# The tail of a four-layer network rearranged: another neighbour for the last convolution, a third of the depthwise chains on ScalarE and GpSimd, more PSUM banks

## The chip, the cores and the metric

The kernel runs on one core of one Trainium2 chip. The metric is the time of one execution on the device in microseconds (us), a median over several runs. Below, a number of a stage comes from the trace of one profiled execution, and a ratio is the mean time of one kernel's fast runs over the mean time of the other's fast runs of the same rounds, so it is not quite the quotient of the two medians quoted beside it. All runs told here were in the fast state, that is, none took over 1.5% longer than the fastest of its kernel on its chip. SBUF is the memory in which the kernel's tiles lie, PSUM the one into which its matmuls write, and a bank is here a PSUM buffer of 512 fp32 numbers for each partition; the granted clock is the share of full speed that the profile records for TensorE.

Three of the four calls for experiments went to chips on which every kernel takes some 1,000 us longer (the kernel before 9792 to 9833 us there, against 8717 to 8729 on the others). Where that time lies can be read in the traces: the part before the tail, with the gathers, ends at about 8100 us instead of 7050, and the last stage of the tail agrees to about 2 us between the chips (208.5 and 208.5 us in two kernels that share it). So every experiment is compared by the lengths of its tail stages, and by its ratio to the kernel before of its own rounds. The same saving in us gives a ratio about a tenth nearer to 1 on a slow chip, and the scatter of the part before the tail, which ended between 8101 and 8137 us in eight profiles on the slow chips, is in every ratio and in no tail.

## The reference, cut to what matters

Four images of 256 channels, 64 x 64 pixels, go through four layers in fp32:

```python
def reference(x, ...):                     # x: (4, 256, 64, 64)
    # layer 0: 1x1 convolution, deformable sampling (gathers), feed-forward
    # layer 1: linear attention over q, k, v and their aggregated copies
    qkv = relu(conv1x1(x) * scale + bias)                 # 768 channels
    agg = depthwise_5x5(qkv) + bias                       # the 25-tap chains
    agg = depthwise_1x1(agg) + bias
    ...                                                   # relu(q), relu(k), v k^T, projection, + x
    # layer 2: 3x3 convolution with binarised weights, + x
    # layer 3: attention over max-pooled keys: theta, phi (1024 keys), softmax, g, projection, + x
    return x
```

Group normalisations stand between the layers, folded into weights. One image depends on no other.

## The kernel before: the parts that matter

Images follow each other through a pipeline. While one image's points are gathered (GpSimd and DMA), another's layer 1 and a third's layers 2 and 3 run on the other engines. Generators yield costs, and `beside` advances several of them in proportion. After the gathers of the last image comes the tail: nothing is left to gather, and image 3 still has its feed-forward part, layer 1, layer 2 and layer 3 to do.

```python
def ps(self, name="ps"):                                   # every small product of TensorE
    return self.mm.tile([P, 512], F32, name=name, tag="mm")   # three PSUM banks rotate
...
def depthwise(self, acc, src, w, k, rows, cols, r0, bias=None, step=...):
    for t in range(k * k):                                 # a chain of 25 taps on VectorE
        s = src[:, r0 + t // k:r0 + t // k + rows, t % k:t % k + cols]
        wt = w[:, t:t + 1]
        if t:
            nc.vector.scalar_tensor_tensor(acc, s, wt, acc, ALU.mult, ALU.add)
        elif bias is not None:
            nc.vector.tensor_scalar(acc, s, wt, bias, ALU.mult, ALU.add)
        ...
        if t % 3 == 2 or t == k * k - 1:
            yield step(3.9)
...
def aggregate(pd, i, name, func, **more):                  # in layer 1, 24 times an image
    acc = self.ps1.tile([P, 16, W], F32, name="agg", tag="agg")     # the one PSUM buffer (two banks)
    yield from self.depthwise(acc, pd, self.w5[:, i], 5, 16, W, 0, bias=..., step=step)
    v = bp.tile([P, 16, W], F32, name=name, tag="ag", bufs=3)
    nc.scalar.activation(v, acc, func, **more)             # the copy that frees "agg"
    yield step(2)
    return v
...
# layer 3, one step of 128 tokens
s = [self.ps("s") for _ in range(2)]
for i in range(2):
    nc.tensor.matmul(s[i], tv[...], ph[...])               # score
    nc.vector.tensor_reduce(mx[:, i:i + 1], s[i], AX.X, ALU.max)
...
    nc.scalar.activation(pe[...], s[i], AF.Exp, bias=mx[:, 2:3], accum_out=...)
...
    nc.tensor.transpose(pt[:, m], pe[...], self.ident)     # then ScalarE copies pt to pT
...
    nc.tensor.matmul(ps[:, 0:P], pT[:, m], gt[:, m], ...)  # product
nc.vector.tensor_scalar(m2[...], ps[:, 0:P], den[:, 2:3], None, ALU.mult)
...
# the tail, in run()
def second(n):
    yield from self.layer2(n, ...)                         # 3x3 convolution
    yield from self.layer3(n, ...)                         # pooled attention
beside(range(64), 64, *behind(N - 1), (second(N - 2), SECOND, 0.2, 1))   # feed-forward and layer 1 of image 3
for _ in second(N - 1):                                                  # ... and then 3's layers 2, 3 alone
    pass
```

## Time and profile before

| kernel before | us |
|---|---|
| median of the runs (8709.94 to 8736.27) | 8729 |
| profiled execution | 8707 |
| of this, tail: end of image 3's feed-forward part to the end | 1669 |
| - layer 1 of image 3, beside layers 2 and 3 of image 2 | 1087 |
| - from there to the last matmul of image 3's convolution | 278 |
| - pooled attention of image 3, alone | 304 |

The borders are the starts of the last matmul of feed-forward's second layer, of layer 1's projection and of the convolution (each of these matmuls takes 0.6 us). Tails are given this way throughout. The prediction uses round borders a few us away (7044, 8150, 8404), so its stages differ by that.

This is the head of the page of the kernel before.

```profile
span 8706.8 us, 92673 instructions
PE 6339.9 (73%) x35276; PEld 3432.2 (39%) x35276; DVE 5243.8 (60%) x6279; ACT 2014.2 (23%) x4710; POOL 4578.5 (53%) x4694
```

No engine is above 73% over the whole, which says little: each stage has its own limit, and only the last fifth of the time is of concern. These groups are of the last stage of the kernel before (window 8404 to 8706). The columns: line, engine, operation, tiles, shapes, count; busy us and mean ns of one; idle time of the engine just before them, and what ended it.

```profile
L963 PE MATMUL ps<-gt,pT 128*128 128x128 f32 x512 | 76.0, 310 | 1.8
...
L958 PE MATMUL pt<-ident,pe 128*128 128x128 f32 x256 | 42.6, 291 | 63.4 <-ACT pe L950 63.0
```

TensorE idles 63 us in front of its transposes, as each waits for the exponentials. The matmuls themselves are recorded at 310 and 291 ns; the number matters later.

### The profile page before, as it was taken

The page shows a single profiled execution, that of the slowest core. Times are in us where ns is not written, and L with a number is a line of the kernel's source. Part 1 is how long each engine was busy: PE and PEld are TensorE (multiplying, and loading weights), DVE is VectorE, ACT ScalarE, POOL GpSimd, SP SyncE. Part 2 cuts the span into 40 slices and gives each one's busy share as a digit, 9 for nine tenths or more (in the row PEclk, how much of TensorE's full clock was granted, in tenths as well). Part 3 has the DMA queues.
Part 4 walks back from the last instruction along what each step waited for, and adds up shares of the span by engine and source line. Part 5 has one row for each costly group of instructions (what it writes and reads, how often), then busy time and mean ns, then how long its engine had stood idle before and what let it go on. Part 6 is the DMA issues. An engine that isn't in the chain of part 4 may idle for free. (4 is left out here: it accounts for less than half of the span.)

```text
span 8706.8 us, 92673 instructions
## 1 busy us (share of the span) xinstructions
PE 6339.9 (73%) x35276; PEld 3432.2 (39%) x35276; DVE 5243.8 (60%) x6279; ACT 2014.2 (23%) x4710; POOL 4578.5 (53%) x4694
## 2 busy tenths in 40 slices
PE   4645545569676677998767779897677898667887
PEld 2333322334333333444444434444444444334345
DVE  7445353342678775258777732778777268989213
ACT  1111111112222122222232322222322222222113
POOL 0667767677777776777776557777755000000000
PEclk7666766779767688999988989998888999889999
DMA  5556555554444454455544354555433211101210
GB/s 157 165 153 170 152 154 157 142 156 144 136 120 127 119 145 136 144 155 140 155 132 119 111 150 137 159 150 152 126 111 107 90 53 46 44 32 41 57 60 29
DMA packets 817660, 1052.57 MB, mean 121 GB/s; under 512 B 464064, under 2 KB 524608, under 8 KB 815424
## 3 DMA queue, kind: packets, MB, share of 16 engines
q0 software_dynamic: 225024, 614.77, 24.4%
q1 hardware_dynamic: 592192, 431.89, 17.3%
q8 instruction: 279, 4.57, 0.2%
q14 instruction: 165, 1.35, 0.0%
HBM read 878.36 MB, written 167.90 MB: 120 GB/s over the span
## 5 line engine op out<-in xcount | busy, mean ns | idle before, releaser
L520 POOL DMA_INDIRECT g<-tab,sl x4688 | 4577.8, 976 | 2169.9 <-issue 1295.2
L176 DVE SCALAR_TENSOR_TENSOR agg<-pad,vec,agg 128x1024 f32<-128x1024 f32 x2560 | 3295.3, 1287 | 69.1
L527 PE MATMUL acc<-g,wm 128*32 128x128 f32 x18752 | 1221.6, 319 | 1186.6 <-ACT at L532 762.0
L527 PEld LDWEIGHTS acc<-g,wm 128*32 128x32 f32 x18752 | 609.5, 121 | 1845.7 <-ACT at L532 984.7
L864 PE MATMUL ps<-xp,w 128*128 128x512 f32 x2304 | 1062.3, 608 | 80.7 <-DVE xp L848 52.8
L864 PEld LDWEIGHTS ps<-xp,w 128*128 128x128 f32 x2304 | 425.7, 192 | 565.5 <-issue 530.8
L552 ACT COPY dT<-dp 64x112 f32<-64x112 f32 x1176 | 287.1, 244 | 1328.9 <-PE dp L537 935.3
L511 DVE TENSOR_TENSOR wm<-con,sl 128x1024 f32<-128x1024 f32 (+1 forms) x296 | 357.5, 1208 | 223.5 <-PE acc L527 221.3
L645 PE MATMUL ps<-x2f,f 128*128 128x512 f32 x1024 | 477.3, 615 | 4.0 <-ACT f L636 4.0
L167 DVE SCALAR_TENSOR_TENSOR hm<-ps,vec,lk 128x512 f32<-128x512 f32 x256 | 192.2, 751 | 436.2 <-ACT lk L166 436.1
L652 PE MATMUL ps<-hm,f 128*128 128x512 f32 x1024 | 453.6, 597 | 0.0
L166 ACT ACTIVATE lk<-ps,low 128x512 f32<-128x512 f32 x320 | 219.8, 687 | 980.9 <-PE ps L645 558.2
L700 PE MATMUL ps<-xr,qw 128*128 128x512 f32 x768 | 418.1, 675 | 12.3 <-DMA xq<-x 3.2
L958 PE MATMUL pt<-ident,pe 128*128 128x128 f32 x1024 | 187.6, 330 | 228.2 <-ACT pe L950 226.1
L950 ACT ACTIVATE pe<-s,mx 128x512 f32<-128x512 f32 x256 | 173.8, 684 | 712.9 <-DVE mx L945 712.8
L414 PE MATMUL ps<-mw,t 128*128 128x108 f32 x512 | 96.5, 364 | 306.9 <-DVE t L404 306.9
L963 PE MATMUL ps<-gt,pT 128*128 128x128 f32 x2048 | 309.6, 314 | 5.6 <-ACT pT L959 3.1
L963 PEld LDWEIGHTS ps<-gt,pT 128*128 128x128 f32 x2048 | 287.9, 224 | 49.4 <-ACT pT L959 20.0
L653 DVE TENSOR_TENSOR xyf<-xyf,ps 128x512 f32<-128x512 f32 x64 | 44.0, 688 | 430.9 <-PE ps L652 430.9
L560 PE MATMUL po<-dT,ow 128*128 128x224 f32 (+1 forms) x1216 | 284.6, 383 | 24.6 <-DVE yb L564 13.2
L532 ACT COPY at<-acc 128x256 f32<-128x256 f32 (+1 forms) x588 | 218.5, 372 | 313.9 <-PE acc L527 304.8
L645 PEld LDWEIGHTS ps<-x2f,f 128*128 128x128 f32 x1024 | 192.1, 194 | 233.2 <-issue 224.5
(224 smaller groups left out, 7096.4 us busy)
## 6 DMA issues: line engine op xcount, KB each, us to landing
x<-x SPq DMA_DIRECT2D x160, 512.0 KB
g<-tab,sl POOLq DMA_INDIRECT x4688
xr<-x SPq DMA_DIRECT2D x96, 512.0 KB
x<-in_x SPq DMA_DIRECT2D x64, 512.0 KB
tab<-xo SPq DMA_DIRECT2D x512, 64.0 KB
y<-yc SPq DMA_DIRECT2D x32, 512.0 KB
x2f<-x SPq DMA_DIRECT2D x32, 512.0 KB
xyf<-x SPq DMA_DIRECT2D x32, 512.0 KB
```

The costliest lines, as they stand in the source:

```text
L166: nc.scalar.activation(t, ps, AF.Identity, bias=low, scale=SLOPE)
L176: nc.vector.scalar_tensor_tensor(acc, s, wt, acc, ALU.mult, ALU.add)
L511: nc.vector.tensor_tensor(wm[:, 0:nu], self.con("own").unsqueeze(1).unsqueeze(1).to_broadcast(sh), sl[:, r:r + nu, G:].unsqueeze(3).to_bro ...
L520: nc.gpsimd.indirect_dma_start(out=g[:, i, :], out_offset=None, in_=table, in_offset=bass.IndirectOffsetOnAxis(ap=sl.bitcast(I32)[:, r, i: ...
L527: nc.tensor.matmul(acc[32 * i:32 * i + 32, :], wm[:, r4, 4 * i + 2 * x:4 * i + 2 * x + 2, :], g[:, i, x * P:(x + 1) * P], start=x == 0, st ...
L552: nc.scalar.copy(dT[b][hs, :, q0:q0 + m * (v1 - v0)].rearrange("p g (v o) -> p g v o", o=m), dp[u][hs, v0:v1, :, s, 0:m].rearrange("p v g ...
L560: nc.tensor.matmul(po[m][:, 0:np_], self.ow[:, k, m * P:(m + 1) * P], dT[b][:, k, 0:np_], start=k == 0, stop=k == G - 1)
L645: nc.tensor.matmul(ps, f1[:, k, m * P:(m + 1) * P], x2[:, k], start=k == 0, stop=k == KT - 1)
L652: nc.tensor.matmul(ps, f2[:, k, m * P:(m + 1) * P], hm[:, k], start=k == 0, stop=k == 4 * KT - 1)
L700: nc.tensor.matmul(ps, qw[:, k, t * P:(t + 1) * P], x[:, k], start=k == 0, stop=k == KT - 1)
L864: nc.tensor.matmul(ps, w[:, k, t, m * P:(m + 1) * P], xp[:, k, t // 3:t // 3 + 8, t % 3:t % 3 + W], start=i == 0, stop=i == KT * 9 - 1)
L963: nc.tensor.matmul(ps[:, 0:P], pT[:, m], gt[:, m], start=m == 0, stop=m == 7)
```

## The change

The intent is to use the tail's idle engines. (1) Image 2's pooled attention no longer runs beside layer 1 but beside image 3's convolution, which had been alone. (2) The sampling's SBUF pools are closed before the tail, which makes room for more buffers. (3) In the tail every third aggregation chain is done by ScalarE (products) and GpSimd (sums). (4) More PSUM banks rotate, and pooled attention in the tail takes its scores in other banks ("wide"). The core of the diff:

```diff
-        return self.mm.tile([P, 512], F32, name=name, tag="mm")
+        tag = next(self.banks)
+        return (self.mm if tag == "mm" else self.ps1).tile([P, 512], F32, name=name, tag=tag)
...
+    def products(self, pool, acc, src, w, k, rows, cols, r0, bias, step):
+        for t in range(k * k):
+            s = src[:, r0 + t // k:r0 + t // k + rows, t % k:t % k + cols]
+            if t:
+                m = pool.tile([P, rows, cols], F32, name="m", tag="product", bufs=4)
+                nc.scalar.activation(m, s, AF.Copy, scale=w[:, t:t + 1])
+                nc.gpsimd.tensor_tensor(acc, acc, m, ALU.add)
+            else:
+                nc.scalar.activation(acc, s, AF.Identity, bias=bias, scale=w[:, t:t + 1])
+            if t % 3 == 2 or t == k * k - 1:
+                yield step(0.5)
...
+                turn += 1
+                if self.alone and turn % 3 == 2:
+                    acc = v = bp.tile([P, 16, W], F32, name=name, tag="av2")
+                    yield from self.products(bp, acc, pd, self.w5[:, i], 5, 16, W, 0, self.b5[:, i:i + 1], step)
+                else:
+                    acc = self.ps1.tile([P, 16, W], F32, name="agg", tag="agg")
...                                                        # pads and "ag": one buffer more when alone
-                    s = [self.ps("s") for _ in range(2)]
+                    if not wide:
+                        s = [self.ps("s") for _ in range(2)]
+                    elif j % 2:
+                        s = self.ps1.tile([P, 2, 512], F32, name="s", tag="agg")
+                        s = [s[:, i] for i in range(2)]
+                    else:
+                        s = [self.ps1.tile([P, 512], F32, name="s", tag=tag) for tag in ("acc", "dp")]
...
-        beside(range(64), 64, *behind(N - 1), (second(N - 2), SECOND, 0.2, 1))
-        for _ in second(N - 1):
+        self.banks, self.alone = cycle(["mm", "acc", "mm", "dp", "mm"]), True
+        beside(range(64), 64, *behind(N - 1), (conv(N - 2), CONV, 0.2, 1))
+
+        self.banks = cycle(["mm", "mm", "mm", "vk"])
+        beside(range(64), 64, (conv(N - 1, "right"), CONV, 0, 1), (pooled(N - 2, True), SECOND - CONV, 0, 1))
+        for _ in pooled(N - 1, True):
             pass
```

More of the change, by code (lines that the diff above doesn't have):

```diff
@@ L41 @@
 LINEAR = 1130
-SECOND = 631
+CONV, SECOND = NB * 32 + 2, 631
 EPS_BN = 1e-5
@@ L74, in __init__ @@
         self.cp = e(tc.tile_pool(name="const", bufs=1, side="left"))
-        self.gp = e(tc.tile_pool(name="gather", bufs=2, side="left"))
-        self.sp2 = e(tc.tile_pool(name="samp", bufs=2, side="left"))
         self.ps1 = e(tc.tile_pool(name="ps1", bufs=1, space=PSUM))
         self.mm = e(tc.tile_pool(name="mm", bufs=3, space=PSUM))
+        self.banks, self.alone = cycle(["mm"]), False
         self.dp = e(tc.tile_pool(name="scratch", bufs=1, space=DRAM))
     def ps(self, name="ps"):
-        return self.mm.tile([P, 512], F32, name=name, tag="mm")
+        tag = next(self.banks)
+        return (self.mm if tag == "mm" else self.ps1).tile([P, 512], F32, name=name, tag=tag)
     def rsqrt(self, pool, v, eps, cols, name):
@@ L182, in depthwise @@
                 yield step(3.9)
+    def products(self, pool, acc, src, w, k, rows, cols, r0, bias, step):
+        nc = self.nc
+        for t in range(k * k):
[8 more added lines that the diff above has]
+                yield step(0.5)
     def setup(self):
@@ L476, in sample @@
     def sample(self, n, ssum):
-        nc, sp = self.nc, self.sp2
+        nc, sp = self.nc, self.sp
         table = self.tab[n].rearrange("g y x s c -> (g y x) (s c)")
@@ L676, in layer1 @@
             nc.vector.memset(ld, 0.0)
-            later = []
+            later, turn = [], 0
+            room = lambda bufs: bufs + self.alone
             def step(cost):
@@ L686, in rows @@
             def rows(tiles, seen):
-                new = lambda c: [self.padded(bp, 1, 20, 2, c, f"pad{i}", bufs=3) for i in range(2)]
+                new = lambda c: [self.padded(bp, 1, 20, 2, c, f"pad{i}", bufs=room(3)) for i in range(2)]
                 pads = {0: new(0)}
@@ L718, in aggregate @@
             def aggregate(pd, i, name, func, **more):
-                acc = self.ps1.tile([P, 16, W], F32, name="agg", tag="agg")
-                yield from self.depthwise(acc, pd, self.w5[:, i], 5, 16, W, 0, bias=self.b5[:, i:i + 1], step=step)
-                v = bp.tile([P, 16, W], F32, name=name, tag="ag", bufs=3)
+                nonlocal turn
+                turn += 1
[4 more added lines that the diff above has]
+                    acc = self.ps1.tile([P, 16, W], F32, name="agg", tag="agg")
+                    yield from self.depthwise(acc, pd, self.w5[:, i], 5, 16, W, 0, bias=self.b5[:, i:i + 1], step=step)
+                    v = bp.tile([P, 16, W], F32, name=name, tag="ag", bufs=room(3))
                 nc.scalar.activation(v, acc, func, **more)
@@ L831, in layer1, with layer2 @@
                 yield step(4)
-    def layer2(self, n, st, st3):
+    def layer2(self, n, st, st3, side="left"):
         nc, tc = self.nc, self.tc
-        with tc.tile_pool(name=f"ca{n}", bufs=1, side="left") as sp, \
-                tc.tile_pool(name=f"cb{n}", bufs=2, side="left") as bp:
+        with tc.tile_pool(name=f"ca{n}", bufs=1, side=side) as sp, \
+                tc.tile_pool(name=f"cb{n}", bufs=2, side=side) as bp:
             w = sp.tile([P, KT, 9, C], F32, name="w2")
@@ L871, in layer2, with layer3 @@
             before.pop()()
-    def layer3(self, n, st):
+    def layer3(self, n, st, wide=False):
         nc, tc, a = self.nc, self.tc, self.a
@@ L976, in run @@
         self.binarise()
-        tile = lambda name, shape, bufs: self.sp2.tile(shape, F32, name=name, bufs=bufs)
-        stats = lambda: {i: tile(f"st{i}", [P, KT, NB, 6], 2) for i in (1, 2, 3)}
-        ssum = [tile(f"ssum{n}", [P, KT, len(BLOCKS)], 1) for n in range(N)]
-        st = {}
-        def feed(n):
-            st[n] = stats()
-            return self.feedforward(n, ssum[n], st[n][1])
-        linear = lambda n: self.layer1(n, st[n][1], st[n][2])
+        tile = lambda name, shape: self.cp.tile(shape, F32, name=name)
+        ssum = [tile(f"ssum{n}", [P, KT, len(BLOCKS)]) for n in range(N)]
+        st = {i: [tile(f"st{i}{n}", [P, KT, NB, 6]) for n in range(2)] for i in (1, 2, 3)}
+        feed = lambda n: self.feedforward(n, ssum[n], st[1][n % 2])
+        linear = lambda n: self.layer1(n, st[1][n % 2], st[2][n % 2])
+        conv = lambda n, side="left": self.layer2(n, st[2][n % 2], st[3][n % 2], side)
+        pooled = lambda n, wide=False: self.layer3(n, st[3][n % 2], wide)
         def second(n):
-            yield from self.layer2(n, st[n][2], st[n][3])
-            yield from self.layer3(n, st[n][3])
+            yield from conv(n)
+            yield from pooled(n)
         def beside(steps, number, *works):
@@ L1015, in run @@
         ordered = lambda: self.tc.manual_schedule(engines={E.PE, E.DVE, E.Activation, E.Pool})
-        with self.tc.tile_pool(name="pw", bufs=1, side="right") as wp, \
-                self.tc.tile_pool(name="pa", bufs=1, side="right") as sp, \
-                self.tc.tile_pool(name="pb", bufs=2, side="right") as bp:
-            w = self.weights(wp)
-            def prepare(images):
-                pads, used = [], []
-                n = len(images)
-                return [((y for i in images for y in self.convolve(i, w, sp, bp, pads, used)), n * CONVOLVE, 0, 1 - 0.12 / n),
-                        (self.shifts(images, w["mw"], bp, pads, used), n * OFFSETS, 0.2 / n, 1)]
-            beside(range(64), 64, *prepare([0]))
-            with ordered():
-                beside(self.sample(0, ssum[0]), rounds, *prepare(list(range(1, N))))
@@ L1033, in run @@
-        behind = lambda n: [(feed(n), FEED, 0, 0.2), (linear(n), LINEAR, 0.2, 1)]
-        with ordered():
-            beside(self.sample(1, ssum[1]), rounds, *behind(0))
-            for n in range(2, N):
-                beside(self.sample(n, ssum[n]), rounds, *behind(n - 1), (second(n - 2), SECOND, 0.2, 1))
-        beside(range(64), 64, *behind(N - 1), (second(N - 2), SECOND, 0.2, 1))
-        for _ in second(N - 1):
+        behind = lambda n: [(feed(n), FEED, 0, 0.2), (linear(n), LINEAR, 0.2, 1)]
@@ new lines, in run, with prepare @@
+        with self.tc.tile_pool(name="gather", bufs=2, side="left") as self.gp, \
+                self.tc.tile_pool(name="samp", bufs=2, side="left") as self.sp:
+            with self.tc.tile_pool(name="pw", bufs=1, side="right") as wp, \
+                    self.tc.tile_pool(name="pa", bufs=1, side="right") as sp, \
+                    self.tc.tile_pool(name="pb", bufs=2, side="right") as bp:
+                w = self.weights(wp)
+                def prepare(images):
+                    pads, used = [], []
+                    n = len(images)
+                    return [((y for i in images for y in self.convolve(i, w, sp, bp, pads, used)), n * CONVOLVE, 0, 1 - 0.12 / n),
+                            (self.shifts(images, w["mw"], bp, pads, used), n * OFFSETS, 0.2 / n, 1)]
+                beside(range(64), 64, *prepare([0]))
+                with ordered():
+                    beside(self.sample(0, ssum[0]), rounds, *prepare(list(range(1, N))))
+            with ordered():
+                beside(self.sample(1, ssum[1]), rounds, *behind(0))
+                for n in range(2, N):
+                    beside(self.sample(n, ssum[n]), rounds, *behind(n - 1), (second(n - 2), SECOND, 0.2, 1))
```

## The prediction

> **What bounds the kernel now.** I read the strip of 40 slices first, to see which stretch the change touches; then the busy times of four stretches of the tail, then the groups of instructions in the two that matter.
>
> ```profile
> DVE  7445353342678775258777732778777268989213
> POOL 0667767677777776777776557777755000000000
> ```
>
> GpSimd is busy with the gathers of the sampling until slice 31 and has nothing to do in the last nine. That is the tail, from about 6800 us to 8706. The order of the instructions on every engine is, but for buffer numbers, the same in both kernels until the feed-forward part of image 3 ends (7044), so nothing before that should move; "sampling's buffers freed" only makes room. The busy times of the tail (columns: PE, PEld, DVE, ACT, POOL, granted clock, DMA share, GB/s):
>
> ```profile
> 6800.00:7044.00 244.00, 224.88 (x526) 100.38 (x526) 73.59 (x120) 50.01 (x74) 0.00 (x0) 0.95 0.25 79
> 7044.00:8150.00 1106.00, 820.49 (x2670) 452.56 (x2670) 924.37 (x1074) 279.15 (x529) 0.00 (x0) 0.87 0.14 44
> 8150.00:8404.00 254.00, 250.49 (x576) 109.80 (x576) 21.61 (x44) 14.53 (x16) 0.00 (x0) 0.98 0.19 51
> 8404.00:8706.00 302.00, 220.41 (x1040) 154.69 (x1040) 98.22 (x256) 108.03 (x232) 0.00 (x0) 0.94 0.14 46
> ```
>
> Row 1 is the feed-forward of image 3, TensorE-bound. Row 2 is layer 1 of image 3 beside the convolution and the pooled attention of image 2: VectorE is busy 924 of 1106 us. Row 3 is image 3's convolution alone, TensorE at 99%. Row 4 is its pooled attention alone: no engine is full, TensorE 220 of 302. The groups of row 2, cut to those used here:
>
> ```profile
> L176 DVE SCALAR_TENSOR_TENSOR agg<-pad,vec,agg 128x1024 f32<-128x1024 f32 x576 | 740.5, 1286 | 10.7
> L864 PE MATMUL ps<-xp,w 128*128 128x512 f32 x576 | 254.9, 595 | 9.6 <-ACT xp L852 9.6
> ...
> L178 DVE TENSOR_SCALAR agg<-pad,vec,b 128x1024 f32<-128x1024 f32 x24 | 32.3, 1346 | 47.1 <-ACT pad L388 25.9 <-ACT pad L710 8.2 <-ACT ak L723 8.0
> ...
> L723 ACT ACTIVATE av<-agg 128x1024 f32<-128x1024 f32 x12 | 12.3, 1024 | 93.4 <-DVE agg L176 93.4
> ...
> L852 ACT ACTIVATE xp<-xp,g_bi,g_r 128x640 f32<-128x640 f32 x12 | 10.9, 919 | 54.8 <-DMA xp<-x 54.7
> ```
>
> 24 aggregation chains of 25 taps take 773 of VectorE's 924 us, with 11 us of idle inside them: they set the length of row 2. Each ends with a copy by ACT out of the one PSUM buffer "agg", and the next chain's first tap cannot start before it. And what holds row 4, as waits:
>
> ```profile
> ACT pe L950 <- DVE mx L945: 141.9, 31, 8.1
> PEld pt L958 <- ACT pe L950: 93.8, 63, 4.7
> DVE m L964 <- PE ps L963: 89.7, 32, 4.7
> ```
>
> Score, maximum, exponential, transpose and product of one 128-token step wait for each other in a ring; only three PSUM banks rotate, so the next score does not start early.
>
> [...]
>
> **The change part by part.**
> Row 2 loses pooled attention of image 2 (98 us VectorE, some 225 TensorE) and 8 of 24 chains. VectorE has left 924 - 98 - 8 x 32.2 = 568 us: 16 chains (515) and 53 us of other work. TensorE: 820 - 225 = 595. [...] ACT: 279 - 115 (pooled) + 8 x 25 products; from 919 ns at 640 elements and 1024 at 1024 out of PSUM I take 1.24 us, so 248, in all 412. By sums alone the stage would be about 620 us plus start and end. [...] In the changed ACT order the products stand in front of the copies that free agg, with four product buffers, so product n waits for GpSimd's add n - 4. Behind chain 1, all 24 products of chain 2 come before the copy of chain 1. Behind chains 4 and 22 the same holds; behind 18, 13 products; and the output copies that chain 19's interleaved VectorE work needs stand behind the end of chain 20.
> I walked this through with [...] 32.7 per VectorE chain and 1.2 per copy. Chain 1 starts at 7061 as before and ends at 7095; the 24th product of chain 2 may go after add 20[...] and the pads of chain 3 come after chain 2's last add at 7122: 29 us of idle. In the same way after chain 4 12, around chains 7 to 10 21, after 13 3, after 18 18, inside 19 21, after 22 17, inside 24 5: together 126 us. Chains 6, 12, 15, 16 are freed in time, since at most 11 to 14 products stand ahead [...].
> Sum: 7061 + 16 x 32.7 (523) + 35 of the other VectorE work inside + 126 + 16 handoffs x 1.5 (24) + 10 of waits for the outputs + 40 for the last chunk's output, where reciprocals (3.35 each) and copies have no chain to hide behind = about 7820. Then a remainder: the generators' cost counters still allow layer 1 its old 1130, though product steps count 0.5 instead of 3.9, so layer 1 runs out early and 75 of image 2's 288 convolution matmuls (TensorE order of the changed kernel) come after its last output: 75 x 2 x 0.435 = 65. End of stage: 7885.
> Convolution of 3 beside pooled attention of 2: TensorE has 250 + 222 = 472 us; VectorE 120 and ACT 130, far below. In the order three convolution matmuls (2.6 us) stand between a score and its transposes, about what maximum (0.69), scalar (0.2) and exponential (0.68 + 0.2) take. I add 10 for the start (normalisation, weights) and 23 for small waits: 505, end 8390.
> Pooled attention of 3 with wide PSUM: scores go one to two steps ahead. TensorE then is the bound: 32 steps x (2.0 score + 1.33 transpose + 2.4 product + 0.5 projection = 6.2) = 198, the first part about 30, the last outputs 10: 238 instead of 302. End 8628, against 8706.8: 79 us less, 0.9%.
>
> So 64 of the 79 us come from the last stage. Rows 2 and 3 cost 1106 + 254 = 1360 before and 841 + 505 = 1346 after: what the lighter chains save is nearly eaten by the stalls, the remainder and the work moved.
>
> **The rivals.**
> (a) VectorE simply gets 257 us less and everything else hides. Then layer 1 ends near 7820 - 126 = 7694 and the kernel near 8500 (-2.4%). [...] Against: the ACT order and four product buffers[...].
> (b) [...] an add costs 3 us: a product chain of 72 us, 8 of them 580, and ACT pinned behind them; layer 1 would end 100 us later and the kernel be at 8730, the same as before. [...]
> (c) Adding the convolution to pooled attention brings TensorE no overlap[...] and the stage costs 250 + 302 = 552: +47, leaving -0.4%. Against: the pieces alternate in small groups.
> (d) The clock: dense fp32 matmuls at 0.98 in row 3 show no throttle, so I give it nothing.
>
> **Range and chances.** The times were 8709.94 to 8736.27; I take the change off the median: 8729 - 79 = 8650. The stalls (126, could be 60 to 200), the mixed stage (480 to 550) and the last (230 to 260) give roughly -85 and +95 together: 8560 to 8735 would hold most; I take 8560 to 8725. Below 8555 (2%) needs most stalls gone: 0.14. Above 8904 needs an unforeseen blockade: 0.02. Within 2%: 0.84.
>
> **What would show each step right or wrong.** The mean of the GpSimd adds [...], and of VectorE's taps beside them (1.286[...]). The idle time before the first tap of a chain: 47 us for 24 before; I expect some 150 for 16, put down to ACT's copies. ACT's products waiting on GpSimd, more than on anything else. TensorE's stretch of pure convolution after layer 1, about 65 us. The mixed stage at 93% or more TensorE. In the last stage, score waits on VectorE nearly gone and 238 us. Wrong it would be if adds take near 1.3 us (rival a), or if anything before 7044 moves.

## The result, and the profile after

The changed kernel took 8658 us (median of 4 runs, 8643.77 to 8663.89), the kernel before 8729. The ratio is 0.992, with a 95% interval of 0.990 to 0.994: 0.8% shorter, and the same within 2%. The outputs were right. A second set of runs on another chip gave 0.9927 (0.9907 to 0.9947).

| us | before | after | difference |
|---|---|---|---|
| layer 1 of image 3 | 1087.0 | 893.5 | -193.5 |
| to the end of its convolution | 277.8 | 505.5 | +227.7 |
| pooled attention of image 3 | 304.0 | 208.5 | -95.5 |
| tail | 1668.8 | 1607.5 | -61.3 |

So the first two rows together, which the change was mostly about, became 34 us longer, and the last stage gives the gain. First the page of the changed kernel: VectorE's and GpSimd's rows in 40 slices.

```profile
span 8661.8 us, 93130 instructions
...
DVE  7445353442677776258787732687778346764224
...
POOL 0667767677777776777776557777665125552000
```

GpSimd now works in the tail, and VectorE, at 8, 9, 8 and 9 tenths in the 34th to 37th slice before, shows 6, 7, 6 and 4. It has less to do, and much of what was taken away came back as idle time. Then the busy times of the stages of the changed kernel, in the columns that the prediction uses (PE, PEld, DVE, ACT, POOL, granted clock, DMA share, GB/s): feed-forward, layer 1, a remainder of image 2's convolution, image 3's convolution beside image 2's attention, image 3's attention.

```profile
6816.00:7057.00 241.00, 228.19 (x537) 103.21 (x537) 71.94 (x108) 50.97 (x78) 0.00 (x0) 0.96 0.23 73
7057.00:7948.00 891.00, 545.10 (x1482) 254.42 (x1483) 598.09 (x599) 388.42 (x493) 451.88 (x192) 0.78 0.11 35
7948.00:8013.00 65.00, 64.93 (x154) 28.56 (x152) 8.13 (x21) 2.52 (x3) 0.00 (x0) 1.00 0.38 113
8013.00:8454.00 441.00, 433.83 (x1618) 251.16 (x1618) 121.29 (x314) 119.45 (x250) 0.00 (x0) 0.99 0.19 59
8454.00:8662.00 208.00, 191.86 (x1040) 146.84 (x1040) 94.34 (x253) 103.48 (x232) 0.00 (x0) 0.97 0.17 59
```

In layer 1, VectorE is busy 598 of 891 us and no engine is full; in the mixture TensorE is busy 98% of the time. In the last stage it is at 92%, where it had been at 73%. The groups of layer 1 (window 7057 to 7948):

```profile
L177 DVE SCALAR_TENSOR_TENSOR agg<-pad,vec,agg 128x1024 f32<-128x1024 f32 x384 | 494.0, 1286 | 10.3
L193 POOL TENSOR_TENSOR av<-av,m 128x1024 f32<-128x1024 f32 x96 | 226.0, 2354 | 399.8 <-ACT m L192 392.6
L192 ACT ACTIVATE m<-pad,vec 128x1024 f32<-128x1024 f32 x192 | 218.0, 1157 | 142.9 <-POOL ak L193 73.9 <-POOL av L193 68.8
...
L179 DVE TENSOR_SCALAR agg<-pad,vec,b 128x1024 f32<-128x1024 f32 x16 | 21.5, 1346 | 89.8 <-ACT av L746 55.2 <-ACT pad L403 17.4 <-ACT ak L746 16.0
```

The taps of VectorE cost 1286 ns beside GpSimd's sums, to the nanosecond what they did alone. GpSimd's adds take 2354 ns. ScalarE's products wait 143 us for GpSimd, yet GpSimd also waits for products: 392.6 us in the line shown, of which 317 lie before its first add. The adds into ak come in as many chains and look the same (2353 ns, 236.5 us of waiting). These are pieces of GpSimd's work in time (start, us, with the idle time before):

```profile
7173.27 58.22 POOL L193 TENSOR_TENSOR ak<-ak,m 128x1024 f32<-128x1024 f32 x24 [32.51 <-ACT m L192]
7264.97 58.33 POOL L193 TENSOR_TENSOR av<-av,m 128x1024 f32<-128x1024 f32 x24 [33.48 <-ACT m L192]
...
7801.75 58.27 POOL L193 TENSOR_TENSOR ak<-ak,m 128x1024 f32<-128x1024 f32 x24 [96.17 <-ACT m L192]
```

Within a chain the four buffers keep GpSimd full, 24 x 2.35 plus handoffs; between chains it stands still for 10 to 96 us, in all 312 (392.6 + 236.5 - 317). It is not the bound of the stage. What VectorE waits for in it (us in total, times, longest):

```profile
DVE pad L392 <- ACT m L192: 73.7, 5, 22.8
DVE agg L179 <- ACT av L746: 55.2, 6, 24.6
DVE x L878 <- PE ps L887: 25.3, 7, 16.8
DVE ot L826 <- ACT ot L825: 18.1, 1, 18.1
DVE ln L796 <- PE vk L771: 17.9, 2, 12.0
```

The first two lines are the products' doing. A pad is a tile of image rows with a border of zeros, which a chain reads; L392 writes zeros into its edge (92 ns of work), and stands in VectorE's order behind ScalarE's products; L179 is a chain's first tap, waiting for the copy out of "agg". Last, the waits of the last stage of the changed kernel (window 8454 to 8662), which answer to the three lines that the prediction shows of before (141.9, 93.8 and 89.7):

```profile
ACT pe L979 <- DVE mx L974: 37.6, 30, 1.5
...
DVE m L993 <- PE ps L992: 30.5, 32, 2.8
```

and two entries of its chain of waits, in order of time (start, us, what), each the product of one step:

```profile
8518.31 1.78 PE ps L992 x16
...
8538.57 1.78 PE ps L992 x16
```

Three more products lie between them, so four steps of 128 tokens take 8538.57 - 8518.31 = 20.26 us, 5.07 each, and the 32 steps 162. All the entries of that stretch are TensorE's: it is the bound now, not the ring.

### The profile page after: what moved, and what is told of

The parts are those of the page before. It is cut to its first block, busy times and chain, and to the rows that moved or that the text cites. A ratio compares the mean times of both kernels' runs of the same rounds, so it can differ in the third digit from the quotient of the medians.

```text
span 8661.8 us, 93130 instructions
## 1 busy us (share of the span) xinstructions
PE 6322.2 (73%) x35276; PEld 3424.4 (40%) x35276; DVE 5020.0 (58%) x6079; ACT 2226.8 (26%) x4910; POOL 5033.6 (58%) x4886
## 5 line engine op out<-in xcount | busy, mean ns | idle before, releaser
L177 DVE SCALAR_TENSOR_TENSOR agg<-pad,vec,agg 128x1024 f32<-128x1024 f32 x2368 | 3049.3, 1288 | 68.8
L887 PE MATMUL ps<-xp,w 128*128 128x512 f32 x2304 | 1081.3, 610 | 66.4 <-DVE xp L871 52.8
L193 POOL TENSOR_TENSOR av<-av,m 128x1024 f32<-128x1024 f32 x96 | 226.0, 2354 | 399.8 <-ACT m L192 392.6
L193 POOL TENSOR_TENSOR ak<-ak,m 128x1024 f32<-128x1024 f32 x96 | 225.9, 2353 | 243.7 <-ACT m L192 236.5
L972 PE MATMUL s<-ph,th 128*128 128x512 f32 x512 | 280.8, 651 | 26.8 <-DVE m L993 8.1
L575 PE MATMUL po<-dT,ow 128*128 128x224 f32 (+1 forms) x1216 | 286.7, 385 | 18.3 <-DVE yb L579 12.5
```

Source lines behind the costliest of these rows:

```text
L193: nc.gpsimd.tensor_tensor(acc, acc, m, ALU.add)
L887: nc.tensor.matmul(ps, w[:, k, t, m * P:(m + 1) * P], xp[:, k, t // 3:t // 3 + 8, t % 3:t % 3 + W], start=i == 0, stop=i == KT * 9 - 1)
L972: nc.tensor.matmul(s[i], tv[:, 4 * b + j], ph[:, i * 512:(i + 1) * 512], start=True, stop=True)
```

## The experiments

My theory after the result had two halves. The gain of the last stage comes from the wide PSUM banks. In layer 1 the 257 us taken off VectorE come back as waits, because the products stand in ScalarE's queue in front of the copies and pads that VectorE needs. The trace of the changed kernel shows it at the first chain: VectorE's last tap ended at 7117.7 us, then six products started, from 7119.0 to 7131.1, with ScalarE idle 1.26 to 1.28 us before each, and the copy out of "agg" started only at 7132.2, behind the last of them. The rivals: that the reordering makes the gain and the products are worth nothing; that GpSimd's pace is the limit; that the remainder of 65 us, or the small number of pads, is the loss.

| run | ratio to before (95%) | layer 1 | to end of convolution | last stage | tail |
|---|---|---|---|---|---|
| changed kernel, again | 0.9927 (0.9907 to 0.9947) | 893.6 | 505.2 | 208.5 | 1607.3 |
| no products | 1.0015 (1.0001 to 1.0029) | 1018.3 | 452.4 | 208.5 | 1679.2 |
| 10 product buffers | 0.9876 (0.9856 to 0.9896) | 855.8 | 505.0 | 208.9 | 1569.7 |
| 6 pads | 0.9931 (0.9908 to 0.9953) | 893.8 | 504.9 | 210.2 | 1608.9 |
| VectorE copies | 0.9916 (0.9890 to 0.9941) | 886.5 | 505.2 | 208.5 | 1600.2 |
| product steps cost 3.9 | 0.9925 (0.9906 to 0.9945) | 943.6 | 450.8 | 209.6 | 1604.0 |
| last stage not wide | 1.0031 (1.0019 to 1.0044) | 893.9 | 504.8 | 297.7 | 1696.4 |
| one after another | 0.9951 (0.9935 to 0.9967) | 894.0 | 318.9 (no attention in it) | 408.6 (both attentions) | 1621.5 |
| old banks in layer 1 | 0.9941 (0.9919 to 0.9962) | 915.5 | 505.9 | 207.7 | 1629.1 |
| ScalarE in program order | 1.0129 (1.0093 to 1.0164) | 1087.7 | 505.0 | 207.6 | 1800.3 |
| the same, 10 buffers | 1.0126 (1.0096 to 1.0156) | 1086.0 | 506.6 | 208.0 | 1800.6 |
| 10 buffers, cost 3.9, VectorE copies | 0.9899 (0.9878 to 0.9919) | 904.3 | 451.0 | 210.4 | 1565.7 |

**The changed kernel again.** No edit; it is the neighbour of three runs below.

> The changed kernel itself again, on the chip of this call, so that the other runs have a neighbour to be compared with. Expected: ratio to before 0.992 (0.989 to 0.995), tail from the end of the feed-forward part to the end 1607 us (within 4), as in its first run.

Tail 1607.3, ratio 0.9927: as in the first run, and stage by stage within 0.5 us. Tails are steady enough to read differences of a few us.

**No products.** The placement, the banks and the buffers remain; all 24 chains are VectorE's again.

```diff
-                if self.alone and turn % 3 == 2:
+                if False:
```

> All 24 chains of the tail on VectorE again, everything else as in the changed kernel (8658 us). Theory W (waits eat the saving: ACT's products stand in VectorE's way): layer 1 gets 257 us of taps back but loses most of its 293 us of VectorE idle, so about 940 to 960 us instead of 891, and the remainder of 75 convolution matmuls (65 us) goes, since the cost counters fit again: 8655 +- 25, about the same as the changed kernel. Rival F (the freed 257 us are worth their full amount): 8850 or more.

Tail 1679 us, 72 more than the changed kernel and 10 more than before. So the products are worth 72 us, and all the rest of the change together nothing (-10). The busy times of its layer 1 show what became of VectorE's relief:

```profile
8123.00:9141.60 1018.60, 619.23 (x1634) 287.75 (x1633) 853.19 (x817) 172.08 (x295) 0.00 (x0) 0.77 0.11 33
```

Without products VectorE is busy 853 us and idle 165; with them busy 598 and idle 293. Of 255 us less work, 128 came back as idle time, and the stage is about 125 shorter. These are VectorE's waits before first taps without the products:

```profile
DVE agg L179 <- ACT ak L746: 14.0, 11, 2.4
DVE agg L179 <- ACT pad L403: 13.0, 2, 9.0
DVE agg L179 <- ACT av L746: 8.3, 9, 1.1
```

With 1.2 us from the pads' other line (L726) they make 36, against 90 with the products; the edges of pads waited for no product here, and 74 us with them. That is 127 us more, so these two kinds of stall hold nearly all that came back. The granted clock is no rival: 0.77 here, 0.78 with the products. Then 53 of the 125 is given back, as the remainder of the convolution grows.

**Ten product buffers instead of four.**

```diff
-                m = pool.tile([P, rows, cols], F32, name="m", tag="product", bufs=4)
+                m = pool.tile([P, rows, cols], F32, name="m", tag="product", bufs=10)
```

> Ten product buffers instead of four: ACT may run ten products ahead of GpSimd, so the last product of a chain goes six adds (14 us) sooner, and so do ACT's copies and the release of the pads. Theory W: 40 to 100 us less than the changed kernel, 8560 to 8620. Rival G (GpSimd's own 8 x 58 us chain or TensorE's order sets layer 1): within 15 us of 8658.

38 us less, with the same instructions on every engine and GpSimd busy 452 us in both, so the limit was not GpSimd's pace. It is a little less than the theory's range. The two waits of VectorE shrink from 129 to 62 us, but others that stand in the same queue grow (L826 from 18 to 34, L179 behind L403 from 17 to 33), so that the stage gains 38 us and not 67:

```profile
DVE agg L179 <- ACT av L746: 38.7, 6, 11.6
DVE ot L826 <- ACT ot L825: 34.1, 2, 27.4
DVE agg L179 <- ACT pad L403: 32.9, 3, 19.8
...
DVE pad L392 <- ACT m L192: 23.4, 5, 8.3
```

**Six pads instead of four.** VectorE's longest wait is a pad's edge behind the products; more pads should free it.

```diff
-                new = lambda c: [self.padded(bp, 1, 20, 2, c, f"pad{i}", bufs=room(3)) for i in range(2)]
+                new = lambda c: [self.padded(bp, 1, 20, 2, c, f"pad{i}", bufs=3 + 3 * self.alone) for i in range(2)]
```

> Six pad buffers per tensor instead of four in the tail, products as they are. The trace of the changed kernel shows 73.7 us in which VectorE's clearing of a pad's edge waits for ACT's products to stop reading that pad. Theory W with the pads as the second half of it: these waits go to zero, part comes back as waits for ACT's copies; 20 to 70 us less, 8590 to 8640. Rival: the next wait takes all of it, 8658 +- 15.

A miss: 1608.9, nothing gained, and the wait is still there:

```profile
DVE pad L392 <- ACT m L192: 61.5, 4, 22.8
```

The compiled order explains it in part. In this stage a scheduler sets the order of the instructions ahead of the run. With six pads it puts the edge fills earlier: counted in the traces, the last one is the 5203rd of VectorE's 6079 busy instructions, instead of the 5288th. So the fill moves forward with the buffer that it may use, and meets the products all the same. That the scheduler misjudges when the products are done is my reading; no run shows it.

**The copies that end VectorE's chains done by VectorE.**

```diff
-                nc.scalar.activation(v, acc, func, **more)
+                if self.alone and v is not acc:      # chains of VectorE in the tail
+                    ...                              # vector max(acc, 0) or copy; a reduce for the sums of k
+                else:
+                    nc.scalar.activation(v, acc, func, **more)
```

> The copies out of the PSUM buffer of VectorE's 16 chains are made by VectorE itself (16 of about 1.1 us, and a sum over 1024 elements for five of them) instead of ACT, so no chain waits for an ACT queue full of products. Theory W: the 71 us of VectorE waiting for those copies go, against 25 us of added work; pads' waits stay: 10 to 50 us less, 8610 to 8650. Rival G: slower by the added 25 us, 8680.

7 us less, under the range expected. The edit gives VectorE 24 us more work in layer 1 (624.5 us busy against 600.1, between the exact borders), and takes 31 us of idle time away. The wait of the first tap on the copy (71 us) is gone, but others take part of its place:

```profile
DVE pad L392 <- ACT m L192: 99.5, 5, 24.1
DVE ot L834 <- ACT ot L833: 42.8, 2, 27.8
```

The copies were not the only thing that VectorE needs from a ScalarE full of products; taking them out moved much of the wait to the next (these two lines held 73.7 and 18.1 us in the changed kernel).

**The cost of the product steps.** The remainder of 65 us exists because product steps count 0.5.

```diff
-                yield step(0.5)
+                yield step(3.9)
```

> The step of a product chain counts 3.9 as the vector steps do, instead of 0.5, so image 2's convolution should spread over the whole of layer 1 and the 65 us of pure convolution after it should go. Theory of the prediction (the remainder is a loss of its own, caused by the cost counter): the remainder falls from 65 to under 10 us and layer 1 grows by little, because TensorE is not its bound there; the tail is 40 to 65 us shorter than the changed kernel's 1607. Rival (the convolution's matmuls, spread, come into the way of the products' handoffs and VectorE's waits; or fewer of them lie where VectorE stalls): the tail is shorter by less than 20 us.

The remainder went from 65 to some 10 us and layer 1 grew by 50: 3 us in all. The rival was right. The wait of the first tap on the copy grew with it (before it was 55.2):

```profile
DVE agg L179 <- ACT av L746: 97.7, 7, 35.6
```

**The last stage without the wide banks.**

```diff
-        for _ in pooled(N - 1, True):
+        for _ in pooled(N - 1):
```

> The last pooled attention (image 3, alone) without the wide PSUM banks: its scores come from the same rotating banks as everything else. Theory of the prediction (the last stage's gain is the PSUM banks that let the next scores start early): the last stage goes from 208 back to about 290 us (the old one was 302), the kernel is 70 to 95 us longer than the changed one, so within 20 us of before. Rival (the ring mm, mm, mm, vk with its fourth bank, and the freed buffers, give most of it): last stage 208 to 240 us.

The last stage goes to 297.7 us, the kernel is 90 us longer than its neighbour (8740 against 8650), and the ring of waits is back:

```profile
ACT pe L979 <- DVE mx L974: 137.4, 30, 8.2
PEld pt L987 <- ACT pe L979: 93.7, 62, 4.5
DVE m L993 <- PE ps L992: 70.5, 32, 4.7
```

So of the last stage's 95.5 us, 89 are the wide banks' in the last stage; the other 6 belong to the rest of the change (the ring of four banks, the buffers), which no run takes apart.

**Convolution and attention one after another.**

```diff
-        beside(range(64), 64, (conv(N - 1, "right"), CONV, 0, 1), (pooled(N - 2, True), SECOND - CONV, 0, 1))
+        for _ in conv(N - 1, "right"):
+            pass
+        for _ in pooled(N - 2, True):
+            pass
```

> Image 3's convolution runs first and image 2's pooled attention after it, one after another, with the same wide PSUM. Theory A (the mixture hides the attention's handoffs under the convolution): convolution alone 254 us, attention alone 208 us (as the last stage), sum 462 and a start of the second, so about 465 to 480 against 441 in the changed kernel: 20 to 40 us longer. Theory B (rival c of the prediction: mixing brings nothing, wide PSUM alone makes attention short): the same within 10 us. Theory C (the step of the mixture in the prediction, where a lone attention was to cost 238 and TensorE 222 of it): 490 or more, over 45 us longer.

14 us longer than the mixture, between the expectations, nearest to the one that gives the mixture nothing. Its stages (layer 1's remainder and the convolution; attention of image 2; of image 3):

```profile
7934.00:8253.00 319.00, 314.54 (x732) 138.82 (x731) 34.84 (x82) 16.90 (x20) 0.00 (x0) 0.99 0.22 63
8253.00:8457.00 204.00, 191.90 (x1046) 146.25 (x1044) 94.58 (x259) 104.89 (x234) 0.00 (x0) 0.98 0.18 62
8457.00:8661.50 204.50, 192.91 (x1036) 147.09 (x1036) 93.13 (x246) 103.30 (x231) 0.00 (x0) 0.96 0.19 63
```

With wide banks an attention alone takes 204 us, TensorE at 94%. There was little left for the convolution to fill.

**The old three banks in layer 1.**

```diff
-        self.banks, self.alone = cycle(["mm", "acc", "mm", "dp", "mm"]), True
+        self.banks, self.alone = cycle(["mm"]), True
```

> The changed kernel with only the three old PSUM banks in the layer-1 stage (the later stages as changed). Theory of the prediction, which gave the banks there nothing: layer 1 893 within 10 us. Rival (the five banks carry part of layer 1's gain, as TensorE, ScalarE and VectorE pass more results there): layer 1 910 to 950 us.

Layer 1 becomes 22 us longer. The prediction had given these banks nothing; they are worth those 22.

**ScalarE in the program's order.** In program order the copy that ends a chain stands before the next chain's products; the scheduler had put the products first.

```diff
-        beside(range(64), 64, *behind(N - 1), (conv(N - 2), CONV, 0.2, 1))
+        with self.tc.manual_schedule(engines={E.Activation}):
+            beside(range(64), 64, *behind(N - 1), (conv(N - 2), CONV, 0.2, 1))
```

> The changed kernel with ScalarE kept in the program's own order in the layer-1 stage, so that the copy that ends a vector chain stands before the products of the next chain, where the scheduler had put all 24 products (or most) before it. Theory of the prediction (VectorE's idle time is due to the products standing in front of the copies and of the pads' fills): VectorE's wait of the first tap on the copy and of the pads' edges on the products (55 + 74 us) mostly go, layer 1 goes from 893 to about 800 to 840 us. Rival (the order is not the point: GpSimd's chain of 58 us has to end in front of the next copy in any in-order ScalarE, so a wait on the product chain's own last copy takes its place): a round of three chains costs 58 + 33 + handoffs, about 95 us, eight of them 760 and the start and end 100 to 130: layer 1 860 to 900 us, no gain.

Neither expectation: layer 1 grows by 194 us. The first tap's wait on the copy is indeed gone from VectorE's list, as the theory said, but worse stands there. VectorE's longest waits, and below them GpSimd's:

```profile
DVE pad L392 <- ACT m L192: 187.3, 5, 52.8
DVE agg L179 <- ACT pad L726: 83.2, 4, 39.8
```

```profile
POOL av L193 <- ACT m L192: 496.1, 4, 347.0
POOL ak L193 <- ACT m L192: 364.4, 4, 96.3
```

GpSimd waits 496 + 364 - 347 = 513 us for products once it has begun, against 312 in the changed kernel: the products now stand behind the copies, which wait 142.5 + 138.8 = 281 us for VectorE's chains (29.9 in the changed kernel), so the two engines take turns. In these two orders, whichever stood first in ScalarE's queue, the other's consumer waited: VectorE 129 us for copies and edges of pads behind products in the one, GpSimd 513 us for products behind copies in the other. The edit fixes the order of everything on ScalarE in this stage, not of the copies alone, so it does not say what moving only these would do. Still, the scheduler's order, with its waits, is far better than the plain one, and "products in front of copies" is not by itself a loss to be removed.

**The same with ten buffers.**

> The same ScalarE order, with ten product buffers instead of four. With four buffers the run of ten saved 38 us of layer 1 in the scheduler's order. Theory of the prediction (products in front of copies): in program order little stands behind the products, so the buffers bring under 15 us more than the same order with four. Rival (GpSimd chain starved or ScalarE held by its pace): 25 us or more.

1086.0 against 1087.7: nothing, as the theory expected. The buffers brought 38 us where the products stand in front of the copies, and 2 where they stand behind them.

**The three edits together.** Ten buffers, steps that count 3.9, and VectorE's copies.

> A try at a better version: ten product buffers instead of four (which alone saved 38 us of the tail), the product steps counted 3.9 (which alone moved the 65 us of convolution left over into layer 1 and lengthened layer 1 by 50, mostly as waits of a chain's first tap for ScalarE's copy, 98 instead of 55 us), and the copies that end the vector chains done by VectorE (which alone took those waits away and saved 7). If the three only add: tail 1607 - 38 - 3 - 7 = 1559 us, about ratio 0.987 to before. If, as the waits suggest, the copies on VectorE take away the very wait that the moved convolution lengthened: tail 1500 to 1545, ratio 0.980 to 0.985. If they get into each other's way (VectorE then carries 16 more copies of 1.3 us and the sums of the keys): tail 1565 or more.

Tail 1565.7 us, 42 under the changed kernel's, where the three alone would add up to 48 and the buffers alone bring 38. By its tail it is 4 us shorter than ten buffers alone (1569.7), by its ratio 0.002 longer, within the intervals: the two can't be told apart. The simplest of the best versions tried is the changed kernel with ten product buffers: 0.988 of the time before, against 0.992 to 0.993.

Two attempts never got to the chip, and no run of them is on record: the build with sixteen product buffers fails for want of SBUF (its message: pool "cb2" asks for 18.3 KB a partition where 1.6 KB are left), and keeping all engines (or VectorE) in program order in layer 1 ends in a deadlock when the program is built. Both were built again when this document was checked, with the same outcome.

## Why the prediction was right, and where it was not

The time (8650 predicted, 8658 measured), the class and the range held. The sum did so because errors cancelled, which is luck. Of the 71 us between the medians the tail holds 61; the rest is scatter of the part before it, which ended 16 us later in the profile of the changed kernel than in that of the kernel before, and only 2 us later in the changed kernel's second profile. So the prediction's sign that nothing before 7044 moves was not met to the letter, but the traces show the same order of instructions on every engine up to there. One slip in its sums: -85 and +95 around 8650 are 8565 to 8745, not 8560 to 8735. The table counts from the end of feed-forward.

| step | predicted us | measured us | error |
|---|---|---|---|
| layer 1 (7044 to 7820) | 776 | 891 | +115 |
| remainder of image 2's convolution | 65 | 65 | 0 |
| convolution beside attention | 505 | 441 | -64 |
| last attention | 238 | 208 | -30 |
| sum | 1584 | 1605 | +21 |

**GpSimd and ScalarE: right.** The pace of an add, on which the prediction's 126 us of stalls rest, was my estimate, and no trace had shown one; in the changed kernel an add took 2.354 us and a chain of 24 took 58.2. A product took 1.157 us against my estimate of 1.24 from two ScalarE instructions of the trace before (919 and 1024 ns). Rival (b) fell: an add took 2.354 us and not 3, and the taps beside the adds stayed at 1286 ns, which I had expected without a run to show it.

**The stalls of the chains: right in size.** I foresaw 126 us of idle and 24 of handoffs, 150; the profile has 90 us before first taps and 74 before pads' edges, 164. The sign that I had named was some 150 us before first taps; pads hold nearly half. Their place was named, their share was not.

**The rest of layer 1: mis-sized, and this is the failed step.** The terms were "35 of the other VectorE work inside + ... 10 of waits for the outputs + 40 for the last chunk's output". My 776 us held 568 of busy VectorE and so 208 idle, 58 of them outside the stalls. The stage had 598 busy and 293 idle, 129 of them outside the stalls: convolution outputs 25, products of linear attention 36 (18 for ScalarE, 18 for TensorE), the matrix of keys and values 18, and 50 in smaller waits. The miss of 115 is thus 30 of work, 14 of stalls and 71 of these other waits. These are not the products' doing. The run without products idles 165 us in layer 1, of which 36 lie before first taps, so 129 lie elsewhere, as many as here; and the kernel before idled 1106 - 924 = 182 us in its row 2, which I had in front of me and did not ask about. Of the 30 us of work, about 10 are small group-normalisation operations that ran beside GpSimd's adds (below). The rest is my subtraction: I took 98 and 773 us, sums of instructions, from a busy time of 924, in which instructions that overlap at their ends count once (their plain sum is 967), so 53 us was left for other work where 82 was measured.

**The remainder: right as a length, wrong as a loss.** It was 65 us. But counted as a cost that a better counter would save, it is worth 3 us: in layer 1 those matmuls lengthen the waits (the first tap's on the copy from 55 to 98 us). Why they lengthen the copies' wait in particular stays open.

**The mixture and the last stage: one mis-sized term.** I read TensorE's cost of one attention off the old stage as 222 us, and 6.2 us a step. The same 1040 matmuls are busy 192 us in the new one, 5.07 us a step. The mean record of a transpose fell from 291 to 276 ns and of a product from 310 to 277, though the scores rose from 615 to 655 (records overlap, so busy time is less than count times mean):

```profile
L972 PE MATMUL s<-ph,th 128*128 128x512 f32 x128 | 73.1, 655 | 0.2 <-DVE mx L973 0.2
L992 PE MATMUL ps<-gt,pT 128*128 128x128 f32 x512 | 63.4, 277 | 0.1
...
L987 PE MATMUL pt<-ident,pe 128*128 128x128 f32 x256 | 34.4, 276 | 3.1 <-ACT pe L979 3.0
```

A part of it is the clock, to which the prediction's (d) gave nothing. The two rows of windows show a granted clock of 0.94 before and 0.97 after. The trace's clock records give TensorE half its clock for 39 us of the old stage, 32 of them busy, and for 12 us of the new one, 9 of them busy. In these stretches a product starts every 213 ns instead of every 112, and all of the 94 products of 512 with records over 385 ns lie in them (8 in the new stage). An estimate from these figures is that half clock cost (32 - 9) / 2, some 11 of the 28 us between 220 and 192. The other 17 are not taken apart, nor is it shown why the old stage had more of these stretches; without the wide banks the granted clock of the last stage is 0.94 again (an estimate from it: 36 of 297.5 us at half clock).

I had used a busy time of a waiting stage as a cost; the two stages show 220 against 192 us for the same work. In the mixture 472 us of TensorE's work became 434, 38 of the -64; the other 26 are the 33 us that I added for the start and small waits, of which 7 appeared. In the last stage it explains all of the -30 (198 became 162; start and end took 46 instead of 40). That more PSUM banks would let the scores go ahead, on which the prediction of this stage rested, is borne out: 208 us with the wide banks, 298 without.

**"So 64 of the 79 us come from the last stage": right in kind, misleading as a cause.** The last stage is 95.5 us shorter and the two before it together 34 longer. But image 2's attention had been hidden under VectorE's chains, and moving it out (with the new banks and buffers) saved 69 us there and cost 175 in the next stage (run without products: 1018 and 452, against 1087 and 278). So placement and banks together are worth -69 + 175 - 95.5 = +10, and the products, -125 in layer 1 and +53 in the remainder, the whole gain of -72. My sum had the same stages and drew the wrong moral: without the products the change is worth nothing.

**The rivals.** (a), all of VectorE's 257 us gained, fell: half of it returned as idle time. (c), no overlap from mixing, is nearly right in effect: the mixture is worth 14 us, since a wide attention alone already fills TensorE to 94%. (d), the clock, is small but not nothing, as said above; and in layer 1 the granted clock fell from 0.87 to 0.78 (0.77 without products). What part that has in the waits for TensorE no run shows.

**A small cost that nobody had counted.** The taps of VectorE kept their 1286 ns beside GpSimd's adds, but some of its smallest instructions did not keep their time. These are VectorE's instructions around the first product chain, with GpSimd adding from 7081.7 on:

```profile
7080.48 0.15 DVE L118 TENSOR_TENSOR g_d<-g_mv,g_mg 128x2 f32<-128x2 f32 x1
7080.60 1.29 DVE L177 SCALAR_TENSOR_TENSOR agg<-pad,vec,agg 128x1024 f32<-128x1024 f32 x1
7081.80 2.28 DVE L119 TENSOR_TENSOR g_d<-g_d 128x2 f32<-128x2 f32 x1
7084.01 1.28 DVE L177 SCALAR_TENSOR_TENSOR agg<-pad,vec,agg 128x1024 f32<-128x1024 f32 x1
7085.20 1.31 DVE L120 TENSOR_TENSOR g_d<-g_d,g_mv 128x2 f32<-128x2 f32 x1
...
7087.63 0.14 DVE L90 TENSOR_SCALAR g_ve<-g_pv 128x2 f32<-128x2 f32 x1
```

An operation on two elements takes 0.15 us before the adds begin, and 2.28 or 1.31 us during them, up to about one add of 2.35. The taps between them, with one SBUF input (1.28 to 1.29 us), the tensor_scalar that reads PSUM (L90, 0.14) and a reciprocal (L93, 0.16) stay as they were. Seven operations of two elements (six with two SBUF inputs and one tensor_scalar with one) took 1.10 to 2.28 us there, some 10 us more in all than before the adds. Why these and not the others, no run shows.

**What stays open.** Which order of ScalarE would be best: the scheduler's holds 129 us in its two longest waits, the program's is 194 us worse, and no version with products and copies interleaved by hand was built. Also open is why the fills of the pads' edges keep their wait with two more pads.

## What to carry to other kernels

Work moved from the bound engine to two idle ones paid here only as far as ScalarE, which stands between them, served both (layer 1 took 893 us in the scheduler's order of its queue and 1088 in the program's): ask what of the bound engine's needs stands behind the moved work in that queue, and give the moved work enough buffers to clear it early (ten for four brought 38 us). Before moving work out of a stage, ask whether it was hidden there: 69 us were saved where it left and 175 paid where it arrived. And take an engine's cost from a stage in which it is the bound, never from the busy time of one in which it waits (222 us were read off such a stage, and 192 measured where TensorE was the bound), and look at the granted clock of both (0.94 and 0.97 here).
